# A message-passing layer on one core: two VectorE duties moved to other iterations, and the layer-1 bias written by ScalarE for four chunks in ten instead of two

## The chip, the core and the metric

The kernel runs on one core of a Trainium2 chip. Its engines are TensorE (in the profile PE for products and PEld for weight loads), VectorE (DVE), ScalarE (ACT), GpSimd (POOL) and SyncE (SP, which issues the transfers). Each has its own list of instructions, and engines wait for one another through semaphores. The metric is the device time of one execution in microseconds. The kernel before takes 597.03 us, the median of three runs (595.70 to 597.55).

## What is computed

There are 128 graphs of 64 nodes with 128 features. For every ordered pair of nodes a message is computed by a three-layer perceptron; messages are masked by the adjacency matrix, summed over the neighbours, and a second perceptron updates the node:

```python
pair = concat(x_i, x_j)                                   # 64 x 64 pairs in each graph
h = relu(pair @ w0 + b0);  h = layernorm(h)
h = relu(h @ w1 + b1);     h = layernorm(h)
m = (h @ w2 + b2) * adj[i, j]
agg = sum_j m
u = mlp_upd(concat(x_i, agg))                             # same form, own weights
out = x + u
```

The adjacency entries are 0 or 1, about one in eight is 1. The kernel computes only the edges that exist, and raises a flag for a dense path if a pair of graphs has more edges than it has slots for (640 slots for each graph) or if an adjacency entry is neither 0 nor 1. The second part of this flag is what the function `odd_weights` prepares.

## The kernel before

**Tiling.** Two graphs form a pair (64 pairs), four pairs a block (16 blocks). The edges of a pair lie in 1280 slots, which are ten tiles of 128 edges. Four tiles are a chunk: 160 chunks, ten in a block. Five chunks, or 20 tiles, form a group `q` (32 groups); the normalisation roots are computed for a group at a time.

**The loop.** One loop of unrolled Python, `for n in range(last + 1)`, writes out the order by hand, since the scheduler is told to keep the program's order. Every iteration has fixed work, and a plan (`at(n, place, fn, ...)`) puts the occasional work into named places of an iteration. The order in an iteration is:

1. places `a` and `m` (small ScalarE and VectorE work),
2. `layer1(n - 8)`: eight products, with the bias, into the only PSUM bank of tile `z`, then the ScalarE instruction that writes `y` = relu(z) (line 579),
3. place `b`,
4. `layer0(n)`: products into `hps`, then ScalarE writes `h` (line 517),
5. `stats0(n - 1)`: four transposes of `h` into the only bank of `hT` (line 523), then four VectorE statistics (line 527),
6. place `k` (`marks`, a product, line 488, and `compare`, line 496),
7. `stats1(n - 8)`: four VectorE statistics of `y` (line 586),
8. places `x`, `x1`, `x2`, `e0`, `e1`, `e`.

The occasional work repeats every ten iterations. Below, the *phase* of an iteration is its number modulo ten.

| phase | occasional work on TensorE | occasional work on VectorE and ScalarE |
|---|---|---|
| 8, 3 | neighbour sums `reduce` (line 655) and `rows` (435, 437) | in 3 before: `odd_weights` (413, 414) and `bias0` (688); in 8 the update's `finish` |
| 9, 4 | none | `rows_hi` (ACT 444), `rows_lo` (DVE 451), `make_tp` (DVE 466) |
| 0 | turns `uh` (700) | `root1`, `inverse_of` (ACT 269, DVE 274) |
| 1 | `u1c` layer (714), `turn_root` (547) | `root_of` (ACT 255, 541; POOL 542) |
| 2, 5 | turns in 5 | update's `layer_out` in 2 |
| 6 | update's first layer (714), `turn_root` (547) | `root_of` |
| 7 | turns `x` (421), `u2c` layer (714) | update's `layer_out` |

**The bias of layer 1.** The normalisation before layer 1 is not applied to `h`; instead the bias is multiplied by the standard deviation of each edge. There are two ways to bring it into the PSUM bank. Normally it is a product of TensorE at line 573 (`z<-b1t,sdT`, 80 rows, 512 columns), ahead of the eight products of the chunk. It needs the transposed deviations `sdT`. For some chunks, `seed(n)` has ScalarE write it beforehand, with four instructions at line 562 of 128 x 128 elements each, which scale the bias row by `SR[q]`, the deviation as it is before the transpose. In the kernel before, the seeded chunks are those with n modulo 5 equal to 1 (30 chunks). `seed(n)` is planned in place `b` of iteration n + 7, behind the `y` of the chunk before, since both use the one bank of `z`.

**The root of a group.** A group's deviations come about in this chain: the statistics of its last chunk (DVE 527, in phase 0 or 5), sums and squares on GpSimd (POOL 245 to 249), the square root on ScalarE (ACT 255) and its rounding (ACT 541), the remainder on GpSimd (POOL 542, tile `sh`), the transpose on TensorE (PE 547, phase 1 or 6), and the copy on ScalarE (ACT 552, `sdT`). `root_of` lies in place `b` of phase 1 or 6, `turn_root` in place `x` of the same iteration.

**The two duties that move.** `odd_weights(b)` is a scalar_tensor_tensor and a reduction over 128 x 256 elements. `bias0` computes the first bias of the update, four instructions of 128 x 128 elements, which nothing needs before `layer_out` in phase 7.

Of the kernel before, what the change touches and what calls it, by code (L numbers as in the profile page):

```python
# [23 lines left out]
def tile_gnn(  # L24
# [40 lines left out]
    nc = tc.nc  # L65
# [9 lines left out]
    QC = QT // CH  # L75
    NCHK = NQ * QC
    PB = 4
    NB = NP // PB
    CPB = NCHK // NB
# [205 lines left out]
    def edge_path(es):  # L285
# [35 lines left out]
        def at(n, place, fn, *args):  # L321
            plan.setdefault((n, place), []).append((fn, args))
# [384 lines left out]
        def layer(u, *pairs):  # L707
            ps = u.bank()
            for q in range(u.n):
                s = slice(q * P, (q + 1) * P)  # L710
                for n, (src, w) in enumerate(pairs):
                    l = (u.blk["xnT"][:, (u.k0 + q) * P:(u.k0 + q + 1) * P] if src == "xn" else
                         getattr(u, src)[:, s])
                    nc.tensor.matmul(ps[:, s], lhsT=l, rhs=w, start=(n == 0),
                                     stop=(n == len(pairs) - 1))
            u.l_ps = ps[:, 0:u.n * P].rearrange("p (q c) -> p q c", q=u.n)
# [44 lines left out]
        L1 = QC + 3  # L761
# [8 lines left out]
        for b in range(NB):  # L770
            o = b * CPB
            if b > 1:
                at(max(o - 25, 0), "a", load_adj, b)
                at(max(o - 12, 0), "a", load_x, b)
            if b > 0:
                r = max(o - 13, 1)
                at(max(o - 14, 0), "m", rank, b)
                at(r, "x", count, b)
                at(r + 1, "a", count_out, b)
                at(r + 1, "a", degrees, b)  # L780
                at(max(o - 9, r + 1), "e", place, b)
                at(max(o - 7, r + 2), "e", place_out, b)
                at(max(o - 7, 13), "m", odd_weights, b)
                at(o - 3, "x", turn_x, b)
                at(o - 2, "a", turn_x_out, b)
            for half, n in ((0, o - 2), (1, o + 3)):
                if n >= 0:
                    at(n, "x2", rows, b, half)
                    at(n + 1, "a", rows_hi, b, half)
                    at(n + 1, "m", rows_lo, b, half)  # L790
        for b in reversed(range(NB)):
            o = b * CPB
            n = o + QC + SC

            if b < NB - 1:
                t = STEADY if b < NB - 3 else LAST[b - NB + 3]
                units = [(Unit(b, 0, PB, nc.gpsimd, ubank), n, t, 0, t[5] - 1)]
                if b == NB - 2:
                    units = [units[0][:3] + (-5, -4)]
            else:  # L800
                units = [(Unit(b, 2, 2, nc.vector, zbank), NCHK + L1 + 1, LAST[3], 1, 1),
                         (Unit(b, 0, 2, nc.gpsimd, hbank), NCHK + L1 - 1, LAST[2], 3, 3)]
            for u, n, t, m0_at, xo_at in units:
                at(n + m0_at, "m", bias0, u)
                at(n + xo_at, "e", residual, u)
                at(n + t[0], "a", sums_out, u)
                at(n + t[1], "x", turn, u, "ysum")
                at(n + t[2], "a", turn_out, u, "ysum")
                at(n + t[3], "x", lambda u: layer(u, ("xn", u0a), ("ysumT", W["w2u"])), u)
                at(n + t[4], "m", layer_out, u, "uh", "m0")  # L810
                at(n + t[4], "e", upd_m0, u)
                at(n + t[5], "x", turn, u, "uh")
                at(n + t[6], "a", turn_out, u, "uh")
                at(n + t[7], "a", upd_root0, u)
                if t is STEADY:
                    for k, q0, q1 in ((0, 0, 1), (1, 1, 2), (2, 2, PB)):
                        at(n + t[7] + k, "x", upd_shift, u, q0, q1)
                else:
                    at(n + t[7], "x", upd_shift, u, 0, u.n)
                at(n + t[8], "x", lambda u: layer(u, ("uhT", W["u1c"])), u)  # L820
                at(n + t[9], "m", layer_out, u, "uy", "usdb")
                at(n + t[9], "e", upd_m1, u)
                at(n + t[10], "x", turn, u, "uy")
                at(n + t[11], "a", turn_out, u, "uy")
                at(n + t[12], "a", upd_root1, u)
                at(n + t[12], "m", upd_inverse, u)
                at(n + t[13], "x", lambda u: layer(u, ("uyT", W["u2c"])), u)
                at(n + t[14], "m", finish, u)

        for n in range(1, NCHK - L1 - 1, QC):  # L830
            at(n + L1 - 1, "b", seed, n)
        for p in range(NP):
            n = p * TG * 2 // CH
            if p > 1:
# [16 lines left out]
        for q in range(NQ):  # L851
            n = q * QC + QC
# [56 lines left out]
        at(0, "a", lambda: place_pair(2))  # L909
        at(1, "m", lambda: place_pair(3))  # L910
        at(1, "a", lambda: turn_x_out_rest())
        at(18, "m", odd_weights, 0)

        def turn_x_out_rest():
            nc.scalar.copy(blocks[0]["xnT"][:, 2 * P:PB * P], blocks[0].pop("x_ps")[:, 2 * P:])
# [65 lines left out]
    with ExitStack() as es:  # L981
        es.enter_context(tc.manual_schedule())
        flag = edge_path(es)
# [160 lines left out]
```

## Time and profile before

| | value |
|---|---|
| time, median of three | 597.03 us |
| span of the profiled run | 594.8 us |
| mean granted TensorE clock | 0.997 |
| PE, PEld busy | 569.8 us (96%), 525.2 us (88%) |
| DVE busy | 479.4 us (81%) |
| ACT busy | 440.1 us (74%) |
| POOL busy | 294.8 us (50%) |
| bias products of line 573 | 126 into `z`, 489 ns each as displayed, and 4 into `hps` |
| ScalarE bias writes of line 562 | 120 (30 chunks), 372 ns each |
| statistics of `hT`, line 527 | 640, 283 ns each |
| `odd_weights` | 16 of 407 ns (413), 16 of 420 ns (414) |
| `bias0` | 64 of 366 ns (688) |

The page has one line for each engine with its busy time, and a line of digits in which each digit is the busy share of one fortieth of the span, in tenths. A group's line gives source line, engine, operation, tiles (written <- read), shapes, count, busy time, mean duration, and the idle time before it with the instruction that ended it. The timeline has the start, the duration (from the first start to the last end where several instructions are merged, as x4), and in square brackets how long the engine had been idle before, and what released it. Durations of consecutive instructions on one engine overlap somewhat, so start-to-start distances, not durations, are what adds up. The ends of TensorE products are modelled, so there too the starts are to be read.

### The profile page before, as it was taken

How to read it: one execution, taken by the hardware profiler on the slowest of the kernel's cores; microseconds unless marked ns; L12 is line 12 of the kernel's file. 1: busy time of each engine (PE TensorE's matmuls, PEld its weight loads, DVE VectorE, ACT ScalarE, POOL GpSimd, SP SyncE). 2: the span in 40 equal slices, each digit the busy share in tenths (PEclk: the TensorE clock that was granted, in tenths of full speed). 3: DMA queues.
4: the chain of work that ended last, by engine and by line, in shares of the span. 5: the costliest groups of instructions: out<-in, count | busy, mean ns of one | idle time of the engine just before them, and what ended most of it. 6: DMA issues, size and time to landing. Idle time of an engine off the chain costs nothing. (4 is left out here: it accounts for less than half of the span.)

```text
span 594.8 us, 15674 instructions
## 1 busy us (share of the span) xinstructions
PE 569.8 (96%) x5363; PEld 525.2 (88%) x5363; DVE 479.4 (81%) x1947; ACT 440.1 (74%) x965; POOL 294.8 (50%) x837
## 2 busy tenths in 40 slices
PE   5888999999999999999999999999999999999894
PEld 4776889999999999999999999999999999999883
DVE  5667788797979889797978979797987979788576
ACT  5687678878868787786868787786878778685434
POOL 1533455554546554463656446365644536446352
PEclk9999999999999999999999999999999999999998
DMA  4664536545544554545453444544354354531201
GB/s 105 158 130 114 114 80 137 110 105 110 120 126 110 131 107 124 91 118 136 110 133 94 123 108 102 148 112 124 90 127 121 91 133 111 106 96 33 52 19 40
DMA packets 91088, 63.87 MB, mean 107 GB/s; under 512 B 57462, under 2 KB 74876, under 8 KB 91004
## 3 DMA queue, kind: packets, MB, share of 16 engines
q1 hardware_dynamic: 90716, 62.69, 45.7%
q8 instruction: 44, 0.72, 0.5%
q14 instruction: 40, 0.33, 0.2%
q10 hardware_dynamic: 288, 0.13, 0.1%
HBM read 6.82 MB, written 4.19 MB: 19 GB/s over the span
## 5 line engine op out<-in xcount | busy, mean ns | idle before, releaser
L527 DVE BATCH_NORM_STATS2 st<-hT 128x6 f32<-128x128 f32 x640 | 141.3, 283 | 55.9 <-PE hT L523 55.8
L576 PEld LDWEIGHTS z<-w1c,h 128*128 128x128 f32 x1248 | 161.5, 191 | 10.7 <-issue 5.0
L576 PE MATMUL z<-w1c,h 128*128 128x128 f32 x1248 | 167.6, 277 | 0.2 <-ACT z L562 0.2
L586 DVE BATCH_NORM_STATS2 st<-y 128x6 f32<-128x128 f32 x640 | 137.6, 278 | 2.7 <-ACT y L579 1.4
L579 ACT ACTIVATE y<-z 128x512 f32<-128x512 f32 x156 | 93.5, 599 | 55.3 <-PE z L576 52.2
L245 POOL TENSOR_TENSOR m_d<-st 128x20 f32<-128x20 f32 x62 | 17.1, 276 | 212.4 <-DVE st L527 189.0
L517 ACT ACTIVATE h<-hps,b0c 128x512 f32<-128x512 f32 x160 | 109.5, 684 | 2.5 <-PE hps L514 2.4
L523 PE MATMUL hT<-ident,h 128*128 128x128 f32 x640 | 97.4, 275 | 1.1 <-DVE st L527 1.1
L642 POOL TENSOR_TENSOR w<-oh,m_q 128x320 f32<-128x320 f16 x126 | 91.4, 742 | 10.1 <-PE hT L523 5.5
L514 PE MATMUL hps<-s,abl 128*128 128x512 f32 (+3 forms) x256 | 92.3, 372 | 0.4 <-ACT h L517 0.4
L523 PEld LDWEIGHTS hT<-ident,h 128*128 128x128 f32 x640 | 76.5, 141 | 11.2 <-ACT h L517 1.3
L514 PE MATMUL hps<-s,abh 128*128 128x512 f32 (+3 forms) x256 | 78.7, 326 | 0.0
L655 PE MATMUL ys<-y,w 128*64 128x128 f32 x1280 | 76.9, 275 | 0.0
L655 PEld LDWEIGHTS ys<-y,w 128*64 128x64 f32 x1280 | 69.2, 137 | 7.0 <-issue 6.6
L573 PE MATMUL z<-b1t,sdT 80*128 80x512 f32 x126 | 61.6, 489 | 0.5 <-ACT y L579 0.2
L496 DVE TENSOR_TENSOR j<-mk,cmpt 128x320 fp32r<-128x320 f32 x126 | 59.8, 475 | 1.6 <-PE mk L488 1.6
L460 ACT ACTIVATE d<-slot,mid 128x640 f16<-128x640 f16 x64 | 53.6, 838 | 0.0
L444 ACT CAST abh<-mu 128x512 fp32r<-128x512 f32 x32 | 18.7, 586 | 44.5 <-PE mu L437 44.5
L514 PEld LDWEIGHTS hps<-s,abl 128*128 128x128 f32 x256 | 49.5, 194 | 1.8 <-ACT i L472 0.9
L514 PEld LDWEIGHTS hps<-s,abh 128*128 128x128 f32 x256 | 49.6, 194 | 0.0
L562 ACT ACTIVATE z<-b1b,m_sd 128x128 f32<-128x128 f32 x120 | 44.6, 372 | 3.9
L472 ACT CAST i<-tp 128x640 fp32r<-128x640 f16 x63 | 45.5, 723 | 1.8 <-DVE tp L466 1.8
(216 smaller groups left out, 1003.7 us busy)
## 6 DMA issues: line engine op xcount, KB each, us to landing
s<-i SPq DMA_DIRECT2D x126, 160.0 KB, 2.7
s<-j SPq DMA_DIRECT2D x126, 160.0 KB, 2.6
xn<-in_x_dram SPq DMA_DIRECT2D x15, 256.0 KB, 3.9
out_dram<-uo SPq DMA_DIRECT2D x15, 256.0 KB, 2.4
an<-in_adj_dram SPq DMA_DIRECT2D x16, 128.0 KB, 2.6
oh<-tp SPq DMA_TRANSPOSE x64, 2.7
xn<-in_x_dram SPq DMA_DIRECT2D x2, 128.0 KB
out_dram<-uo SPq DMA_DIRECT2D x2, 128.0 KB
```

The source lines that it names most:

```text
L460: nc.scalar.activation(D[p], slot, AF.Abs, bias=blocks[b]["mid"][:, q:q + 1], scale=-1.0)
L496: nc.vector.tensor_tensor(JR[p][:, c], MK.pop((p, k))[:, 0:HC], cmpt[:, c], op=ALU.is_equal)
L514: nc.tensor.matmul(ps[:, c:c + w], lhsT=ab[:, g % 4, :], rhs=s, start=(k == 0), stop=(k == 1))
L517: nc.scalar.activation(H[n], ps, AF.Relu, bias=b0c)
L523: nc.tensor.transpose(ps[:, t, :], H[n][:, t * P:(t + 1) * P], ident)
L527: nc.vector.bn_stats(ST0[q][:, CH * c + t, :], ps[:, t, :])
L573: nc.tensor.matmul(ps, lhsT=SD[q], rhs=W["b1t"][:, CH * c:CH * c + CH, :], start=True, stop=False, skip_group_check=True)
L576: nc.tensor.matmul(ps[:, t, :], lhsT=h[:, t * P:(t + 1) * P], rhs=W["w1c"], start=False, stop=True, skip_group_check=True)
L579: nc.scalar.activation(Y[n], ps, AF.Relu)
L586: nc.vector.bn_stats(ST1[q][:, CH * c + t, :], Y[n][:, t, :])
L642: (nc.vector if p == NP - 2 else nc.gpsimd).tensor_tensor(WT[p][:, :, g, :], OH[p][:, :, g * N:(g + 1) * N], Q[q][:, k:k + TG].unsqueeze(2 ...
L655: nc.tensor.matmul(YS[b][g * N:(g + 1) * N, k, :], lhsT=w[:, t, g, :], rhs=y, start=(t == 0), stop=(t == TG - 1))
```

## The change

Three duties get other places. `odd_weights` of block b moves from phase 3 (iteration 10b - 7) to phase 0 (10b - 10), with special cases for the first three blocks: blocks 0, 1, 2 go from iterations 18, 13, 13 to 10, 20, 30. `bias0` moves four iterations ahead, from phase 3 to phase 9, for all blocks but the last two. And `seed` is done for the chunks with n modulo 10 in (0, 1, 6, 9), instead of (1, 6): 60 chunks and not 30. The new ones, 0 and 9, have their ScalarE writes in phases 7 and 6. The purpose is to take work off TensorE, giving it to ScalarE, and to have the VectorE duties where VectorE is less loaded.

```diff
-                at(max(o - 7, 13), "m", odd_weights, b)
+                at(o - 10 if b > 2 else 10 + 10 * b, "m", odd_weights, b)
...
-                units = [(Unit(b, 0, PB, nc.gpsimd, ubank), n, t, 0, t[5] - 1)]
+                units = [(Unit(b, 0, PB, nc.gpsimd, ubank), n, t, -4, t[5] - 1)]
...
-        for n in range(1, NCHK - L1 - 1, QC):
-            at(n + L1 - 1, "b", seed, n)
+        for n in range(1, NCHK - L1 - 1):
+            if n % CPB in (0, 1, 6, 9):
+                at(n + L1 - 1, "b", seed, n)
...
-        at(18, "m", odd_weights, 0)
+        at(10, "m", odd_weights, 0)
```

The first of these lines is in the loop over the blocks (o = 10b), the second fixes when `bias0` of a block is planned (its fourth entry), the third plans the ScalarE bias, and the last is block 0. In the order of VectorE's list, `bias0` comes to stand between `rows_lo` and `make_tp` of phase 9, and `odd_weights` between the statistics of `y` of phase 9 and `inverse_of` of phase 0. In ScalarE's list, the four writes of phase 6 come between `y` and the square root of `root_of`; those of phase 7 come between `y` and `h`.

## The prediction

> **What bounds the kernel now.** I read the page's busy lines and slices first, then the waits of the weight loads in the steady part (110 to 500 us), then one block of ten iterations in the timeline, engine by engine.
>
> ```profile
> PE 569.8 (96%) x5363; PEld 525.2 (88%) x5363; DVE 479.4 (81%) x1947; ACT 440.1 (74%) x965; POOL 294.8 (50%) x837
> ...
> PE   5888999999999999999999999999999999999894
> ```
>
> TensorE is full from about 75 us to 535 us; only the start and the end are loose. [...] That is 88% here, and 18.5 to 19.0 us of nearly every 20 us in the steady windows, so the verdict stands: what TensorE waits for, or stops doing, is the time. Its waits in the steady part:
>
> ```profile
> PEld ys L655 <- issue: 5.5, 23, 0.2
> PEld z L576 <- issue: 3.9, 23, 0.2
> PEld z L573 <- ACT y L579: 3.2, 12, 0.3
> ```
>
> These repeat once a block or more. Twelve times, once a block, the bias product waits about 0.27 us for `y`; this is phase 1. The 23 "issue" gaps of 0.17 us stand before chunks whose bias ScalarE has written. [...] A block takes 34.36 us: `turn_root` of phase 6 starts at 302.31 and again at 336.67.
>
> The stretches that the change touches, VectorE in phases 9 and 0:
>
> ```profile
> 312.43 0.69 DVE L451 TENSOR_TENSOR abl<-mu,abh 128x512 fp32r<-128x512 f32 x1 [1.91 <-ACT abh L444]
> 313.04 0.38 DVE L466 TENSOR_SCALAR tp<-d,deg 128x640 f16<-128x640 f16 x1
> 313.79 0.89 DVE L527 BATCH_NORM_STATS2 st<-hT 128x6 f32<-128x128 f32 x4 [0.38 <-PE hT L523]
> 314.60 0.86 DVE L586 BATCH_NORM_STATS2 st<-y 128x6 f32<-128x128 f32 x4
> 315.93 0.28 DVE L274 RECIPROCAL m_q<-m_sq 128x20 f32<-128x20 f32 x1 [0.47 <-ACT m_sq L269]
> 316.12 0.82 DVE L527 BATCH_NORM_STATS2 st<-hT 128x6 f32<-128x128 f32 x4
> ```
>
> The 1.91 us of idle time lie *ahead* of `abl`; behind it there are only 0.38 and 0.47 us up to the statistics of phase 0, which end the group. From those the root chain runs on; phase 1, then ScalarE in phase 6:
>
> ```profile
> 319.16 0.27 POOL L542 TENSOR_TENSOR sh<-m_sd,sh 128x40 fp32r<-128x40 f32 x1
> ...
> 319.71 0.27 PE L547 MATMUL ma<-ident,sh 128*80 128x128 f32 x1
> ```
>
> ```profile
> 333.94 0.60 ACT L579 ACTIVATE y<-z 128x512 f32<-128x512 f32 x1 [0.38 <-PE z L576]
> 334.51 0.31 ACT L255 ACTIVATE m_sd<-m,eps_c 128x20 f32<-128x20 f32 x1
> 334.85 0.22 ACT L541 CAST sh<-m_sd 128x40 fp32r<-128x40 f32 x1
> 334.98 0.68 ACT L517 ACTIVATE h<-hps,b0c 128x512 f32<-128x512 f32 x1
> 335.56 0.71 ACT L472 CAST i<-tp 128x640 fp32r<-128x640 f16 x1
> 336.98 0.26 ACT L552 CAST sdT<-ma 80x128 fp32r<-80x128 f32 x1 [0.70 <-PE ma L547]
> ```
>
> Where `turn_root` had to wait (at 45.80, 63.26 and 80.56 us) it started 0.05 us after `sh` of GpSimd ended. So in phase 1 it could have started at 319.48 and has 0.23 us of slack; in phase 6 `sh` ends at 335.54, and the slack is 1.08 us.
>
> [...]
>
> **Part 1, 30 bias products less.** With the product, layer 0 starts 1.13 us after the bias product's start (306.06 to 307.19, 336.70 to 337.83); a chunk without it takes 0.92 us (311.69 to 312.61). That is 0.21 us each, not the displayed 489 ns. Chunks n = 9 wait for one semaphore in the new order, and save 0.21. Chunks n = 0 wait for two, as the present ones do, so the 0.17 us gap takes back part: between 0.04 and 0.21, and I take 0.12. Upper bound of the gain: 30 x 0.21 = 6.3 us; with my values 15 x 0.33 = 5.0 us.
>
> **Part 2, ScalarE's writes in phase 6.** `y` at 333.94; the writes start 0.64 later and take 1.52 start to start (323.95 to 325.47), so the square root moves from 334.51 to 336.10, its rounding to 336.44 to 336.66, `sh` on a then idle GpSimd to about 336.74 to 337.01, and `turn_root` from 336.67 to 337.06. Behind it on TensorE lies the whole of phase 7. Cost 0.39, less Part 1's 0.21 and 0.12: **+0.06 us a block**. Each engine here is behind the writes alone, so this sum is fairly firm.
>
> **Part 3, the writes in phase 7.** `y` comes 0.17 later, at 338.28; the writes end at about 340.50. TensorE is ready for the next chunk at 340.60. Hidden, by a margin of 0.1 us; this is the thinnest one. The copies behind them (`xnT`, `d`) come 1.5 us later and `y` of phase 8 0.6 us later, but phase 8 is 5.6 us long (306.06 to 311.69), with `reduce` and `rows` covering it, and ScalarE idles 1.52 us at its end. Cost 0.
>
> **Part 4, the duties leave phase 3.** There they take 1.82 us of VectorE (324.39 to 326.21). TensorE is in `reduce` and `rows` until 327.5, and the next reader, `hT` of phase 4, comes at 329.00 while VectorE's statistics are done at 327.09. `abl` of phase 4 starts at 328.27, when `abh` of ScalarE has just ended (328.24). Gain 0.
>
> **Part 5, the duties arrive in phases 9 and 0.** `bias0` takes 1.04 start to start (325.17 to 326.21) and sits behind `abl`: `tp` moves from 313.04 to 314.08 and ends at 314.45; ScalarE's `i` waits for it, 314.24 to 314.47, and with it all of ScalarE's queue, so `y` of phase 0 is 0.23 later and TensorE's existing wait of phase 1 grows by 0.23. The statistics of phase 9 start at 314.42, those of `y` at 315.23, `odd_weights` takes 0.78 (324.39 to 325.17) from 316.02, the reciprocal follows at 316.80, and the statistics of phase 0 at 316.99 instead of 316.12: +0.87. GpSimd, ScalarE and `sh` follow by the same 0.87. `turn_root` of phase 1: 319.48 + 0.87 = 320.35 instead of 319.71, **+0.64 us**, which includes the 0.23. VectorE is behind until phase 2 and catches up in phase 3. The full pair occurs in 11 blocks (`odd_weights` in iterations 40, 50, ... 140): 7.0 us, plus 0.2 for the last `bias0` alone at iteration 149.
>
> **Part 6, the start.** Here `turn_root` waits already, so delays count in full. Iteration 11: `odd_weights` of block 0 uses up 0.48 us of idle time ahead of the statistics at 42.37, +0.24. Iteration 16: +1.59 by the writes of ScalarE, less 0.21 and 0.12. Iteration 21: one `bias0` and two `odd_weights`; statistics from 77.12 to 79.05, +1.93. Iteration 26: square root from 95.30 to 96.46, slack 0.65 gone, +0.37 less 0.33. Iteration 31: two `odd_weights`, statistics +1.66, less 0.23 slack, +1.43. The work that leaves iterations 13 and 18 held nobody: idle time stands behind it. Sum +4.9 us.
>
> **Sum:** 7.2 + 12 x 0.06 + 4.9 = 12.8 us; 597.0 + 12.8 = **609.8, I say 610 us**.
>
> **The rivals.**
> - *Spare time is real, only TensorE's list counts.* For it: DVE is at 81% and ACT at 74%, and I have not seen this order run. Then 30 products less give 3.7 to 6.3 us: 592 us. Against it: the slack after `abl` is 0.85 us for 1.82 us of work.
> - *Half of it.* The chain absorbs most of Part 5, or the start recovers what it loses, because the root is needed only two iterations later, and later work on TensorE gets shorter. Then 2 to 6 us stay: 601 us.
> - *The writes of phase 7 come too late.* The margin is 0.1 us; if ScalarE reaches them 0.5 us later than I say, each of 12 blocks pays up to 0.5 us more: 616 us.
>
> **How the numbers follow.** My case (603 to 613) 0.62, half 0.13, late writes 0.09, spare time 0.16. Faster is the spare-time case: 0.16. Within 0.3% (595.2 to 598.8) is a small part of "half": 0.05. Slower: 0.79. The range from 598 to 616 leaves out the spare-time case and the edges.
>
> **What would show it.** Right: about 96 bias products on `z`; `turn_root` waiting for `sh` of GpSimd some 25 times or more, in total 10 us or more; a block of about 35.05 us; the statistics of phase 0 following `odd_weights` without idle time; busy PE down. Wrong: few waits at `turn_root`, a block shorter than 34.36, or waits of `z` for line 562, which would be the late writes. If `odd_weights` in phase 0 shows idle time on both sides, Part 5 fails.

## The result and the profile after

The change makes the kernel slower: 610.89 us, the median of four runs (610.23 to 611.66), against 596.37 us of the kernel before on the same chip (594.19 to 597.55). The ratio is 1.0248, with a 95% interval of 1.0214 to 1.0283. The profiled runs have spans of 610.0 and 594.8 us.

The page of the kernel after, its busy line and the slices of TensorE and of its clock:

```profile
PE 573.7 (94%) x5333; PEld 521.6 (86%) x5333; DVE 477.9 (78%) x1947; ACT 480.7 (79%) x1085; POOL 289.6 (47%) x837
...
PE   5898889999999999999999999999999999999895
...
PEclk9989989999999999999999999999999999999999
```

There are 30 products fewer (5333 after 5363), yet the share of TensorE falls. The time of its weight loads falls too, from 525.2 to 521.6 us, or from 88 to 86% of the span; in before they were busy for 18.3 to 19.0 of every 20 us from 110 to 490 us. Work left TensorE, and more idle time came in. The slices show that part of it lies in the start: slices 5 and 6 are 8, where they were 9 before. In the line of the granted clock two digits are 8, a matter that comes back below.

The waits of the weight loads in the steady part (110 to 515 us; what waited, for what, then total us, times, longest):

```profile
PEld ma L547 <- POOL sh L542: 9.2, 23, 1.0
PEld ys L655 <- issue: 5.5, 23, 0.2
PEld z L573 <- ACT y L579: 4.5, 12, 0.4
PEld hT L523 <- DVE st L527: 4.5, 13, 0.4
PEld z L576 <- issue: 4.1, 24, 0.2
```

The first line is new: `turn_root` waits for the root 23 times, about twice a block, where in this stretch it had never waited. The wait of phase 1's bias product for `y` has grown from 3.2 to 4.5 us in the same twelve times. The waits of `hT` for the statistics belong to the same late stretch of VectorE. No line says that `z` waits for ScalarE's writes.

VectorE in phases 9 and 0, the same stretch as was shown of before:

```profile
323.62 0.69 DVE L451 TENSOR_TENSOR abl<-mu,abh 128x512 fp32r<-128x512 f32 x1 [1.91 <-ACT abh L444]
324.23 1.13 DVE L688 SCALAR_TENSOR_TENSOR m<-c2u,deg,ub0b 128x128 f32<-128x128 f32 x4
325.27 0.38 DVE L466 TENSOR_SCALAR tp<-d,deg 128x640 f16<-128x640 f16 x1
325.57 0.88 DVE L527 BATCH_NORM_STATS2 st<-hT 128x6 f32<-128x128 f32 x4
326.37 0.85 DVE L586 BATCH_NORM_STATS2 st<-y 128x6 f32<-128x128 f32 x4
327.14 0.41 DVE L413 SCALAR_TENSOR_TENSOR a<-an 128x256 f32<-128x256 f32 x1
327.58 0.42 DVE L414 TENSOR_REDUCE nball<-a 128x1 f32<-128x256 f32 x1
327.92 0.27 DVE L274 RECIPROCAL m_q<-m_sq 128x20 f32<-128x20 f32 x1
328.10 0.82 DVE L527 BATCH_NORM_STATS2 st<-hT 128x6 f32<-128x128 f32 x4
```

The idle 1.91 us ahead of `abl` is still there: `bias0`, placed behind it, starts 0.61 us after it and uses none of it. Behind `abl` no idle time is left. From `abl` to the statistics of phase 0 it was 3.69 us and is now 4.48.

ScalarE in phase 6 of the kernel after:

```profile
345.72 0.60 ACT L579 ACTIVATE y<-z 128x512 f32<-128x512 f32 x1 [0.37 <-PE z L576]
346.35 1.58 ACT L562 ACTIVATE z<-b1b,m_sd 128x128 f32<-128x128 f32 x4
347.87 0.30 ACT L255 ACTIVATE m_sd<-m,eps_c 128x20 f32<-128x20 f32 x1
348.20 0.22 ACT L541 CAST sh<-m_sd 128x40 fp32r<-128x40 f32 x1
```

and what follows from it on GpSimd and TensorE:

```profile
348.50 0.27 POOL L542 TENSOR_TENSOR sh<-m_sd,sh 128x40 fp32r<-128x40 f32 x1 [1.41 <-ACT sh L541]
...
348.82 0.31 PE L547 MATMUL ma<-ident,sh 128*80 128x128 f32 x1 [0.21 <-POOL sh L542]
```

The four writes stand between `y` and the square root, and the root reaches TensorE too late. In phase 1 the same two lines stand 0.32 us apart, at 331.15 and 331.47.

A block takes 34.89 us, after 34.36 (from `turn_root` to `turn_root` ten iterations later). Between the starts of layer 0, phase by phase, only these stretches differ in the steady part; the two halves of a stretch are divided by `turn_root` of phase 6:

| stretch | change, us | predicted | why |
|---|---|---|---|
| phase 0 to 1 | +0.24 | +0.23 | bias product waits for `y` |
| phase 1 to 2 | +0.37 | +0.41 | `turn_root` waits for `sh` |
| phase 6 to its `turn_root` | +0.37 | +0.39 | `turn_root` waits for `sh` |
| `turn_root` to layer 0 of phase 7 | -0.19 | -0.21 | no bias product |
| phase 7 to 8 | -0.24 | -0.12 | no bias product |
| sum (the block itself differs by 0.53) | +0.55 | +0.70 | |

The 15.2 us between the spans lie as follows: 8.8 between `turn_root` of iterations 6 and 31 (90.76 after 81.92), 6.2 from there to iteration 151 (418.35 after 412.12), 0.4 from 151 to 161, and -0.2 ahead of iteration 6. So more than half of the loss is in the start, in about a seventh of the iterations.

### The profile page after: what moved, and what is told of

Same layout as the page of the kernel before. It is cut to its first block, busy times and chain, and to the rows that moved or that the text cites. A ratio compares the mean times of both kernels' runs of the same rounds, so it can differ in the third digit from the quotient of the medians.

```text
span 610.0 us, 15737 instructions
## 1 busy us (share of the span) xinstructions
PE 573.7 (94%) x5333; PEld 521.6 (86%) x5333; DVE 477.9 (78%) x1947; ACT 480.7 (79%) x1085; POOL 289.6 (47%) x837
## 5 line engine op out<-in xcount | busy, mean ns | idle before, releaser
L245 POOL TENSOR_TENSOR m_d<-st 128x20 f32<-128x20 f32 x62 | 15.5, 250 | 226.1 <-DVE st L527 204.4
L523 PE MATMUL hT<-ident,h 128*128 128x128 f32 x640 | 99.3, 278 | 1.1 <-DVE st L527 1.1
L562 ACT ACTIVATE z<-b1b,m_sd 128x128 f32<-128x128 f32 x240 | 89.2, 371 | 7.8
L523 PEld LDWEIGHTS hT<-ident,h 128*128 128x128 f32 x640 | 76.0, 142 | 14.5 <-DVE st L527 5.7
L451 DVE TENSOR_TENSOR abl<-mu,abh 128x512 fp32r<-128x512 f32 x32 | 22.1, 692 | 53.8 <-ACT abh L444 53.7
L573 PE MATMUL z<-b1t,sdT 80*128 80x512 f32 x96 | 47.3, 493 | 2.4 <-ACT y L579 0.6
```

Of the source, the lines that this page charges most:

```text
L523: nc.tensor.transpose(ps[:, t, :], H[n][:, t * P:(t + 1) * P], ident)
L562: nc.scalar.activation(Z[n][:, t, :], W["b1b"], AF.Copy, scale=SR[q][:, k:k + 1])
```

## The experiments

The theory was the prediction's: VectorE and ScalarE carry the root's chain in a fixed order, so a piece of work costs what it exceeds the slack behind it, whatever the engine's busy share. The rivals: the pieces cost in proportion to their length, or one of the parts is free and only one does harm. "Block" and "start" below are the distances just named; before has 34.36 and 81.92. The diffs are against the kernel before unless it says otherwise.

### The parts alone

`odd_weights` and `bias0` moved, the seeds as before:

```diff
-at(max(o - 7, 13), "m", odd_weights, b)
+at(o - 10 if b > 2 else 10 + 10 * b, "m", odd_weights, b)
...
-units = [(Unit(b, 0, PB, nc.gpsimd, ubank), n, t, 0, t[5] - 1)]
+units = [(Unit(b, 0, PB, nc.gpsimd, ubank), n, t, -4, t[5] - 1)]
...
-at(18, "m", odd_weights, 0)
+at(10, "m", odd_weights, 0)
```

> Both VectorE duties moved as in the change, the ScalarE bias as before (30 chunks). My theory (the two together use up more than the slack behind abl): block of ten iterations 34.36 + 0.61 = 34.97 us, of which 0.24 in the wait of the bias product for y in phase 1 and 0.37 in the wait of turn_root in phase 1; about 3.6 us more at the start (iterations 11, 21, 31); 607 us in all. Rival (the duties go into spare time, and it is the ScalarE writes that cost): block 34.36, 596.5 us.

Measured: 605.87 us, ratio 1.0171 (1.0147 to 1.0195); block 34.97, start 84.83. In the steady part only two stretches differ from before, phase 0 to 1 by +0.25 and phase 1 to 2 by +0.37, just those of the change. The waits of its weight loads, as above:

```profile
PEld ma L547 <- POOL sh L542: 4.9, 12, 1.0
PEld z L573 <- ACT y L579: 4.5, 12, 0.4
```

`turn_root` waits once a block now, not twice: this is the phase 1 half. The duties alone cost 0.61 us a block. Their start loses 2.9 us, where about 3.6 were expected.

The seeds alone:

```diff
-for n in range(1, NCHK - L1 - 1, QC):
-    at(n + L1 - 1, "b", seed, n)
+for n in range(1, NCHK - L1 - 1):
+    if n % CPB in (0, 1, 6, 9):
+        at(n + L1 - 1, "b", seed, n)
```

> ScalarE writes the bias for the four chunks of ten, the VectorE duties as before. My theory: turn_root of phase 6 comes 0.37 later, the two products left out give back 0.43, so block 34.30 us; about 1.2 us lost at the start (iteration 16), in all 597 us, no change. Rival (the writes carry the loss of the change): block above 34.8, 607 us. Second rival (the writes are hidden, only TensorE's list counts): block 33.93, 590 us.

Measured: 597.72 us, ratio 1.0047 (1.0028 to 1.0065); block 34.29, start 84.75. The waits, with the other half of the change's and the old wait for `y` unchanged:

```profile
PEld ma L547 <- POOL sh L542: 4.7, 12, 0.4
...
PEld z L573 <- ACT y L579: 3.1, 12, 0.3
```

Its stretches are -0.19, -0.24 and +0.37, so one wait of 0.37 a block uses up nearly all that the missing products give. The start, 2.8 us longer where about 1.2 were expected, makes it a loss; what was left out of the 1.2 is found below, under the start.

`bias0` alone and `odd_weights` alone (the second and the other two hunks of the first diff):

> bias0 alone moved to phase 9, odd_weights and the ScalarE bias as before. My theory: the statistics of phase 0 come only 0.2 later, inside the slack of turn_root; what is left is tp and y of phase 0, 0.23 us a block: block 34.59, 599.5 us. Rival (each duty costs in proportion to its length, 1.04 of 1.82 us of the 0.61): block 34.71, 601 us.

Measured: 599.30 us, ratio 1.0059 (1.0040 to 1.0077); block 34.61, start 82.57.

> odd_weights alone moved, bias0 and the ScalarE bias as before. My theory (slack used up first): it fits into the 0.47 us ahead of the reciprocal and the 0.23 us at turn_root but for 0.01, so block 34.37 us although 0.78 us of VectorE work is new there; the start loses some 2.5 us in iterations 11, 21 and 31, 598 us in all. Rival (the 0.61 of both is shared by length): block 34.36 + 0.26 = 34.62 us, 601 us.

Measured: 597.45 us, ratio 1.0035 (1.0021 to 1.0049); block 34.38, start 83.69.

The sum of the two alone is 0.25 + 0.02 = 0.27 us a block; together they cost 0.61. `odd_weights`, 0.78 us of VectorE, is free in the steady part as long as nothing else has used up the slack, and costs some 0.36 when `bias0` has. This is how slack behaves and not how a cost in proportion to length does. (The start of `odd_weights` alone loses 1.8 us, for some 2.5 expected.)

### The order instead of the amount

The change's seeds, with the loop that plans them set behind the loop that plans `root_of`. In place `b` of phase 6 the square root then comes ahead of the four writes. The diff is against the seeds alone:

```diff
-for n in range(1, NCHK - L1 - 1):
-    if n % CPB in (0, 1, 6, 9):
-        at(n + L1 - 1, "b", seed, n)
...
 for q in range(NQ):
...
+for n in range(1, NCHK - L1 - 1):
+    if n % CPB in (0, 1, 6, 9):
+        at(n + L1 - 1, "b", seed, n)
```

> As the run before, but in phase 6 the square root and its rounding stand ahead of the four writes on ScalarE. My theory: turn_root waits no more, both products' time is won: block 34.36 - 0.43 = 33.93 us, 590 us in all. Rival (the writes, now 0.5 us later, come too late for the layer 1 of phase 7): the wait moves from turn_root to the first product of z, block 34.3, 596 us.

Measured: 592.39 us, ratio 0.9955 (0.9931 to 0.9978); block 33.89, start 84.59. ScalarE in phase 6:

```profile
331.99 0.60 ACT L579 ACTIVATE y<-z 128x512 f32<-128x512 f32 x1 [0.38 <-PE z L576]
332.56 0.31 ACT L255 ACTIVATE m_sd<-m,eps_c 128x20 f32<-128x20 f32 x1
332.90 0.22 ACT L541 CAST sh<-m_sd 128x40 fp32r<-128x40 f32 x1
333.03 1.58 ACT L562 ACTIVATE z<-b1b,m_sd 128x128 f32<-128x128 f32 x4
```

and TensorE behind it:

```profile
334.72 0.27 PE L547 MATMUL ma<-ident,sh 128*80 128x128 f32 x1
334.83 1.06 PE L576 MATMUL z<-w1c,h 128*128 128x128 f32 x8
```

`turn_root` starts without idle time, and the writes end at 333.03 + 1.58 = 334.61, 0.22 us ahead of the products that need them. The same number of writes now costs nothing in the steady part, and the 0.47 us a block of 34.36 - 33.89 is the full gain of two bias products.

The same for VectorE: the duties of the first experiment, with `bias0` of the moved kind put into place `a`, which comes ahead of `abl`. The diff is against that experiment:

```diff
-at(n + m0_at, "m", bias0, u)
+at(n + m0_at, "a" if m0_at == -4 else "m", bias0, u)
```

> Both duties moved as in the change, but bias0 stands ahead of rows_lo on VectorE (place a instead of m in the same iteration); ScalarE bias as before. My theory: bias0 falls into the 1.91 us in which VectorE waits for abh, so that only odd_weights is left: block 34.37 us, against 34.97 with bias0 behind abl. Rival (what counts is the amount of work in phases 9 and 0, not its place): block 34.97 us.

Measured: one run of 596.76 us; block 34.38, start 83.67. VectorE in phase 9:

```profile
310.52 1.12 DVE L688 SCALAR_TENSOR_TENSOR m<-c2u,deg,ub0b 128x128 f32<-128x128 f32 x4
312.51 0.69 DVE L451 TENSOR_TENSOR abl<-mu,abh 128x512 fp32r<-128x512 f32 x1 [0.87 <-ACT abh L444]
313.12 0.38 DVE L466 TENSOR_SCALAR tp<-d,deg 128x640 f16<-128x640 f16 x1
313.88 0.89 DVE L527 BATCH_NORM_STATS2 st<-hT 128x6 f32<-128x128 f32 x4 [0.38 <-PE hT L523]
```

The idle time ahead of `abl` shrinks from 1.91 to 0.87 us by just the length of `bias0`, and the 0.38 us behind `tp` are back. Ahead of `abl` in the list, `bias0` starts 1.99 us before it; behind it in the list, 0.61 us after it, with VectorE idle for 1.91 us until `abl` starts. Block 34.97 becomes 34.38, the value of `odd_weights` alone. The same four instructions cost nothing on one side of a waiting instruction and, with `odd_weights` behind, 0.59 us on the other.

Both orders together in the changed kernel (its diff, with these two):

> The whole change with two orders swapped: in phase 6 the root ahead of the ScalarE bias, in phase 9 bias0 ahead of rows_lo. My theory: the two repairs add up, block 33.90 us, so 1.0 us less than the change; start as costly as with the change but for the two waits at turn_root, 594 to 597 us. Rival (the repairs collide, as ScalarE and VectorE are both later): block above 34.2 us, 600 us.

Measured: 595.63 us, ratio 1.0005 (0.9988 to 1.0022); block 33.92, start 88.59. The whole steady loss is gone, and 0.44 us a block is gained. Over twelve blocks that is 5.3 us, but the start is longer, and the time is that of before. The profile is of an execution of 598.06 us, 2.4 us above the median; its start is 6.7 us longer, 5.3 of it between iterations 16 and 21, where TensorE had half its clock from 65 to 72 us (the mean granted clock of that profile is 0.992).

### The start

The whole change once more, without an edit, to see what of the start recurs:

> The changed kernel once more, for a second profile of its start. If the two half-clock stretches of the first profile (about 31 to 34.5 and 86 to 89 us) belong to the change's longer waits at turn_root, they come back at the same iterations (6 and 21), and the turn of iteration 31 is again 90.8 us after that of iteration 6. If they are chance, they lie elsewhere or are missing, and the distance is nearer to 87.5 us.

Measured: one run of 610.21 us; block 34.88, start 89.26. The start differs from that of the first profile in one stretch: from iteration 6 to 11 it takes 14.37 us, in the first profile 15.85; the four other stretches of five iterations agree within 0.02. What differs there is TensorE's granted clock. First the kernel after in four windows, then this one in two (window, length, busy us of PE, PEld, DVE, ACT, POOL with counts, clock, DMA share, GB/s):

```profile
28.00:32.00 4.00, 2.04 (x13) 1.70 (x13) 2.87 (x10) 1.93 (x6) 3.42 (x8) 0.89 0.29 70
32.00:36.00 4.00, 4.00 (x23) 3.61 (x22) 1.28 (x5) 2.36 (x8) 2.31 (x3) 0.69 0.95 248
...
84.00:88.00 4.00, 2.61 (x13) 2.52 (x14) 2.27 (x11) 2.13 (x6) 3.92 (x9) 0.71 0.34 81
88.00:92.00 4.00, 4.00 (x32) 3.71 (x33) 2.44 (x11) 3.06 (x6) 1.11 (x5) 0.86 0.52 124
```

```profile
28.00:32.00 4.00, 1.88 (x13) 1.55 (x14) 3.02 (x11) 1.93 (x7) 3.27 (x8) 1.00 0.32 77
...
84.00:88.00 4.00, 3.94 (x20) 3.84 (x21) 1.19 (x7) 2.71 (x6) 3.23 (x7) 0.60 0.66 162
```

The kernel after has two stretches in which the granted clock is 0.50, from 31.08 to 34.49 and from 85.69 to 89.11 us, 3.41 us each; outside of them it is 1.00 from 20.84 us, where its record begins, to 607.93 us. (A mean of 0.71 over 4 us is 2.3 us at half clock, 0.86 is 1.1 us.) The second profile has only the later one. The first begins 0.29 us ahead of the start of a `turn_root` that had waited, the later one 0.30 us behind such a start. But the wait of iteration 6 isn't the change's: all twelve profiles, that of before among them, have it with 1.95 to 1.97 us, and only one has the half clock behind it. The later one is at `turn_root` of iteration 21, right after a wait of 1.69 us (0.63 in before):

```profile
85.39 0.31 PE L547 MATMUL ma<-ident,sh 128*80 128x128 f32 x1 [1.69 <-POOL sh L542]
...
85.82 1.91 PE L576 MATMUL z<-w1c,h 128*128 128x128 f32 x8
```

Eight products that take 1.06 us elsewhere take 1.91 here. A clock of 0.50 over 3.41 us is a loss of up to 1.7 us, an estimate from these two numbers; it fits the 1.5 us by which the start differs between the two profiles.

The other part of the start is a wait that the prediction had put at nothing. TensorE's waits from 62 to 75 us in the kernel after:

```profile
PE ma L547 <- POOL sh L542: 2.0, 1, 2.0
PE z L576 <- ACT z L562: 0.7, 1, 0.7
```

The second line is layer 1 of chunk 10 in iteration 18, which waits for ScalarE's writes of iteration 17. In the steady part the `u2c` layer (351.49 to 352.46) stands ahead of those products and covers the writes; in iteration 17 there is no update yet, and nothing does. The first `u2c` layer comes in iteration 37, so chunk 20 meets the same wait in iteration 28:

```profile
107.35 1.16 PE L576 MATMUL z<-w1c,h 128*128 128x128 f32 x8 [0.70 <-ACT z L562]
```

A last one, of 0.5 us, is in iteration 158: there the `u2c` layer stands ahead, but `marks` and the turns of `x`, which other blocks have there too, are over.

The root-first seeds meet the same waits, and one more. TensorE's waits from 60 to 82 us in that kernel:

```profile
PE mu L203 <- ACT beb L202: 1.6, 1, 1.6
PE ma L547 <- POOL sh L542: 1.0, 2, 0.6
PE z L576 <- ACT z L562: 0.7, 1, 0.7
```

Before had the second line in this window too, with the same numbers, but not the first and the third. `beb` is a small table of the update; one of its four copies by ScalarE falls into iteration 16, now behind the writes. So the root-first order should lose little if the first two of the new seeds, chunks 9 and 10 (written in iterations 16 and 17), are left out. The diff is against the root-first seeds:

```diff
-    if n % CPB in (0, 1, 6, 9):
+    if n % CPB in (0, 1, 6, 9) and n not in (9, 10):
```

> As e3_seeds_root_first, but the new ScalarE bias starts at chunk 19: chunks 9 and 10 keep TensorE's product. My theory: block 33.89 as there, and the 1.9 us that e3 loses between the turns of iterations 16 and 21 (17.30 us before, 19.18 there) are not lost: 590 us in all, ratio 0.990. Rival (that loss is another one, of the clock or of the transfers): the same 592.4 us.

Measured: 590.82 us, the median of six runs (589.34 to 591.28), ratio 0.9911 (0.9888 to 0.9934); block 33.89, start 82.67. This is faster than the kernel before and the kernel after. From iteration 16 to 21, where the root-first seeds took 19.18 us after 17.30 of before, it takes 17.28, and neither of the two waits is left. The 0.75 us that the whole start is still longer lie between iterations 26 and 31 (17.29 us after 16.50 of before): there ScalarE still writes chunks 19 and 20, and the weight loads wait for these writes twice, 1.2 us in all. The page of this run:

```profile
PE 563.9 (96%) x5335; PEld 519.8 (88%) x5335; DVE 479.0 (81%) x1947; ACT 475.9 (81%) x1077; POOL 294.7 (50%) x837
```

TensorE has lost 28 products and 5.9 us of busy time, and this time nothing came in their place.

Last, the change with its start left as before: the moved duties and the new seeds begin no earlier than iteration 36.

```diff
-at(max(o - 7, 13), "m", odd_weights, b)
+at(o - 10 if b > 4 else max(o - 7, 13), "m", odd_weights, b)
...
-units = [(Unit(b, 0, PB, nc.gpsimd, ubank), n, t, 0, t[5] - 1)]
+units = [(Unit(b, 0, PB, nc.gpsimd, ubank), n, t, -4 if b > 1 else 0, t[5] - 1)]
...
-for n in range(1, NCHK - L1 - 1, QC):
-    at(n + L1 - 1, "b", seed, n)
+for n in range(1, NCHK - L1 - 1):
+    if n % CPB in ((0, 1, 6, 9) if n > 28 else (1, 6)):
+        at(n + L1 - 1, "b", seed, n)
```

> The change from iteration 36 on (ScalarE bias from chunk 29, bias0 from block 2, odd_weights from block 5); the start as in the kernel before. My theory (the time of the change is a steady part of 0.53 us a block and a start of about 8 us): blocks of 34.89 us, the distance of the turns of iterations 6 and 31 is 81.9 us as before, 602 us in all. Rival (the start costs little, and later blocks carry the loss): 608 us or more.

Measured: 601.87 us, ratio 1.0127 (1.0094 to 1.0160); block 34.90, start 81.94. The start is that of before, the block that of the change. It is 6.4 us longer than the kernel before as measured beside it (595.51). So of the 14.5 us about 6.4 are those of the later iterations and about 8 the start's, in agreement with the division by iterations above (6.2 + 0.4, and 8.8 or, in the second profile, 7.3).

## Why the prediction was right, step by step

The direction, the size (610 forecast, 610.89 measured) and the mechanism held: the duties behind `abl` and the writes ahead of the square root each make `turn_root` wait. That the sum came within 1 us is in part luck: two terms were off in opposite directions, the steady part too high, the start too low.

- **Part 1, products less.** Predicted 0.21 for chunks 9 and 0.12 for chunks 0. Measured 0.19 and 0.24. The second was halved on the assumption that the 0.17 us gap of the other seeded chunks would appear there. It did not: the "issue" waits of line 576 are 24, and were 23 before. The value taken lay in the middle of the bounds 0.04 and 0.21; the upper one was right. Over twelve blocks this is 1.4 us, about what the steady part was put too high.
- **Part 2, writes in phase 6.** +0.37 measured for +0.39. The root-first order, which removes it and nothing else, shows that it is the place ahead of the square root.
- **Part 3, writes in phase 7.** Cost 0 holds in the steady part: the writes there end at 350.69 + 1.58 = 352.27, the products start at 352.46. It fails in iterations 18 and 28, by 0.7 us each, and in iteration 158 by 0.5. The step that failed is that it was worked out for a block with all its work of phase 7 and used for blocks without. The rival "late writes", one such wait in every block, did not come.
- **Part 4, leaving phase 3.** In the change and with the duties alone, no stretch between phases 2 and 6 has become shorter; gain 0 is right.
- **Part 5, duties in phases 9 and 0.** The statistics of phase 0 moved by 0.79 us against `abl` for +0.87 predicted, and phases 0 to 2 grew by 0.61 for 0.64. `odd_weights` runs with no idle time on either side. That the two costs don't add up (0.27 us alone, 0.61 together) is what shared slack implies and a cost by length doesn't.
- **Part 6, the start.** Predicted +4.9; measured +8.8 in one profile and +7.3 in the other. This is the mis-sized term. The steps of Part 6, set between the turns that they delay, against the second profile (the first has +1.66 in the first row):

| from `turn_root` of | predicted | measured | what the difference is |
|---|---|---|---|
| 6 to 11 | +0.24 | +0.19 | |
| 11 to 16 | +1.59 | +1.20 | work that left iteration 13 had held TensorE |
| 16 to 21 | +1.60 (1.93 - 0.33) | +2.20 | wait of 0.7 in iteration 18 |
| 21 to 26 | +0.37 | +1.98 | half clock |
| 26 to 31 | +1.10 (1.43 - 0.33) | +1.77 | wait of 0.7 in iteration 28 |
| sum | +4.90 | +7.34 | |

The work of iteration 13 did not hold "nobody": in before TensorE waits there for `u1c`, a table that VectorE computes behind two `odd_weights`:

```profile
52.67 0.32 PE L435 MATMUL mu<-w0a,xnT 128*64 128x128 f32 x1 [0.53 <-DVE u1c L184]
```

With `odd_weights` alone moved this wait is gone, and the stretch from 11 to 16 is 0.37 us shorter. From 21 to 26 the duties alone add 0.00 and the seeds alone 0.36, both at full clock (1.00 from 76 to 92 us with the duties alone), as predicted. The 1.6 us more of the change fit the up to 1.7 us of the half-clock stretch that lies there, and the first profile's other one cost 1.5 us by the comparison of the two profiles.
- **The sum.** By the prediction, 7.2 + 0.7 us in the blocks and 4.9 in the start; measured, 6.2 + 0.4 and 8.8 (7.3 in the second profile).

What was to show it: the bias products on `z` are 96, as said. `turn_root` waits for `sh` of GpSimd in 30 weight loads, 18.2 us of the whole run, for at least 25 times and 10 us said. The block is 34.89, not 35.05. One sign was badly chosen: "busy PE down" is true of the share (96 to 94%) and of the weight loads (525.2 to 521.6 us), but the busy time of products rose from 569.8 to 573.7 us though there are fewer. In part this is because products that ran at half clock are displayed longer (eight of them 1.91 us for 1.06): the second profile, with one such stretch less, shows 572.0.

The rival "spare time is real" had the gain of the products right, and its forecast of 592 us is what the root-first seeds measure. Its error is to count an engine's free time without asking on which side of a waiting instruction it lies.

## What to carry to other kernels

On an engine that works its list in order, as VectorE did here (1.91 us idle ahead of `abl`, with `bias0` next in the list), look for the idle time ahead of the instruction that waits and the slack behind it: the same work was free ahead of `abl` and cost up to 0.59 us a block behind it. Where new work meets a chain that another engine waits for, put the chain's short instructions first: with 0.5 us of square root and rounding ahead of 1.5 us of writes, a slower variant became a faster one. Cost the start of a pipeline separately, since cover that each steady block has can be missing there (0.7 us in iterations 18 and 28), and an edit that pays in the steady part is best begun only when the cover exists.

## What the runs showed of the hardware that was not expected

**Short waits and TensorE's clock.** The clock that TensorE was granted took two values in the kernel after, 1.00 and 0.50, and its two stretches at 0.50 in the start lasted 3.41 us each. The stretch with half the clock in the changed kernel with both orders, from 65 to 72 us, is about twice as long. The later stretch of the kernel after follows the wait of 1.69 us in iteration 21. In the 3.41 us ahead of it, which hold that wait, TensorE was busy for about half of the time, 1.72 us, and its weight loads for 1.16:

```profile
82.28:85.69 3.41, 1.72 (x13) 1.16 (x12) 3.41 (x16) 1.84 (x5) 2.59 (x8) 1.00 0.01 4
```

Three other profiles (the duties alone, `odd_weights` alone, the duties with `bias0` ahead of `abl`) have this same wait with the full clock around it, 1.00 in each window of 4 us from 76 to 92 us. These are the two windows around it with the duties alone:

```profile
76.00:80.00 4.00, 2.96 (x21) 2.09 (x18) 3.93 (x17) 1.97 (x5) 1.06 (x5) 1.00 0.34 82
80.00:84.00 4.00, 2.77 (x23) 2.68 (x24) 2.51 (x12) 3.20 (x8) 3.92 (x9) 1.00 0.37 91
```

For the first stretch the comparison is with before. In the kernel after TensorE was busy for 1.41 us, and its weight loads for 1.07, of the 3.41 us ahead of this stretch (27.67 to 31.08 us). In before, the 3.41 us up to the same point of the wait of iteration 6, 0.29 us ahead of the start of `turn_root`, have the same two numbers, and the clock behind them is 1.00:

```profile
27.92:31.33 3.41, 1.41 (x9) 1.07 (x9) 3.18 (x12) 1.34 (x5) 2.52 (x8) 1.00 0.40 97
31.33:34.74 3.41, 3.12 (x23) 2.86 (x24) 1.28 (x5) 3.08 (x10) 3.23 (x5) 1.00 0.67 177
```

So the length of the wait doesn't tell these profiles apart, nor, in iteration 6, does the busy time just ahead. What gave half the clock in one and not in the other was not shown: no run moved a wait alone. Several of the experiments' profiles also had a half-clock stretch ahead of iteration 6, and a lower mean granted clock with it (0.988 with the duties alone, 0.990 with the change from iteration 36 on; 0.997 in before, where the record of the clock begins at 20.64 us); the distances above leave it out.

**A second semaphore without a gap.** Chunks 0 were expected to pay 0.17 us ahead of their first weight load, as other seeded chunks do (in before 23 times from 110 to 515 us, 3.9 us in all). There the saving of a product was 0.24 us with no new gap, though the separate semaphore instructions of 51 ns at line 576 went from 30 to 45, one more for each of the 15 chunks 0 and none for chunks 9; the products of chunks 0 come behind the `u2c` layer. Why the gap is absent there was not tried.
